# Layer 1 of a two-layer graph kernel: the last chunk's split on GpSimd, group stores at a fixed place, separate tiles for drained halves, a shorter last group

## The chip, the cores and the metric

The kernel runs on one core of a Trainium2 chip. The metric is the device time of one execution, in microseconds (us). A core has TensorE (PE in the profile) for matrix products, with its weight loads (PEld) beside them, VectorE (DVE), ScalarE (ACT) and GpSimd (POOL) for elementwise work, and SyncE (SP), which here only issues DMAs. Each engine works through its own queue in order and waits on semaphores for the others. PSUM is the memory that TensorE writes to[...].

## The reference

Two layers act on 4096 rows of 512 numbers, with a 4096 x 4096 adjacency matrix `adj` that weighs edges and masks them. Layer 0 is attention with the adjacency added to the logits; the change doesn't touch it. Layer 1 is a graph attention with 8 heads of 64:

```python
nX = (x @ W).reshape(n, NHEAD, OUT_DIM).transpose(1, 0, 2)
mean = nX.mean(-1, keepdims=True)
std = jnp.std(nX, axis=-1, ddof=1, keepdims=True)
nX = a_ln * (nX - mean) / (std + EPS) + b_ln
at1 = jnp.einsum('kno,ok->kn', nX, a1)[:, :, None]
at2 = jnp.einsum('kno,ok->kn', nX, a2)[:, :, None]
kg = at1 + at2.transpose(0, 2, 1)
kg = jax.nn.leaky_relu(kg, negative_slope=LK_ALPHA)
kg = kg * graph[None, :, :]
mg = jnp.where(mask[None, :, :], kg, NEG_FILL)
attention = jax.nn.softmax(mg, axis=-1)
y = attention @ nX + nX
y = y.transpose(1, 0, 2).reshape(n, NHEAD * OUT_DIM)
return jax.nn.elu(y)
```

Here `graph` and `mask` are `adj`, and `x` is the output of layer 0 after a layer norm and a maximum with 0. The result is added to the output of layer 0.

## The kernel before

The kernel computes both layers on a fast path without a running maximum in its softmaxes, checks ranges at the end, writes an integer `flag`, and branches to a general path if the check fails (lines 74 and 75). In the runs here the branch passes the general path by.

Layer 1 has two parts. In the first, 32 blocks of 128 rows are normalised, turned and projected (`turn`, `project`); `variance` and `standardize` divide by the deviation and give nX, the sums at1 and at2, and `own`, the rows to be added later. After each chunk of four blocks, `split` adds a constant to the sums and cuts each into three bf16 pieces, so that a product of two bf16 operands can later form at1 + at2; `sides` and `fours` turn the pieces and store them (z1_d, z2_d, u4_d). Deviations need a power -1/2, which GpSimd computes roughly, and which `standardize` refines on VectorE by five small operations. The last chunk's split doesn't fit in the first part: `split_last` spreads its 14 operations over steps 2 to 8 of the second part, two at the end of a step, and `standardize(31)` runs in the middle of step 0.

The second part is a loop of 512 steps: 8 chunks of 512 target rows (`ic`), two groups of four heads (`hg`), 32 blocks of source rows (`jt`). A group is 32 steps. Everything wrapped in `seq` stays in the order in which the program lists it, on every engine; what is not wrapped is placed by a scheduler. In step n TensorE forms the logits of the right and left heads (`sums`, lines 881 and 911; `left_sums`, line 891), VectorE and GpSimd weigh them with the adjacency (`right_leaky` 929, `right_weigh` 935, `left_weigh` 938), ScalarE takes exponentials of step n - 2 (942), and TensorE multiplies those of step n - 4 by nX (`values`, 950), into the accumulators `accs`: one tile of two halves.

Every fourth step `load_adj` issues the loads for four steps ahead on SP: pieces z2, masks nb and nx, and the weights g. Ten steps before a group ends, `open_group` loads the next group's z1 and u4, and `load_u4` the second half of u4 six steps before its end.

At the end of a group `finish` copies the two halves of `accs` to a tile `ob`, one on ScalarE and one on VectorE (965, 966), and over the next steps turns them to rows (976), divides (988, 989), adds the own rows by an accumulating DMA (1003), splits into a negative and a positive part on GpSimd, takes the exponential, and adds two more times by DMA. `close` (1018) stores the rows 21 steps after `finish` was called, that is at the end of step 24 of the next group. It isn't wrapped in `seq`.

The last group can't hide this work. For it `finish` loads the own rows and the layer's input rows to `last_in` beforehand and adds them on VectorE (1041 to 1047), in two halves with two stores (1048). Then the range check follows, not in `seq`: reductions, comparisons, two transposes on TensorE, and `flag` (1357 to 1377).

Of the kernel before, what the change touches and what calls it, by code (L numbers as in the profile page):

```python
# [24 lines left out]
SB = 4  # L25
# [54 lines left out]
def fast_path(  # L80
# [723 lines left out]
    with tc.tile_pool(name="ga_g", bufs=2) as adjs, tc.tile_pool(  # L804
# [149 lines left out]

        def finish(n, ic, hg):

            grp = groups.pop((ic, hg))
            ob = work.tile([P, 2, GC], F32, name="ob", tag="ob", bufs=1)
            y = work.tile([P, SB, 2, 2, HD], F32, name="y", tag="y", bufs=1)

            def room():
                grp["e"] = work.tile([P, SB, 2, 2, HD], F32, name="e", tag="ob", bufs=1)

            def copies():
                seq(nc.scalar.copy(ob[:, 0, :], accs[:, 0, :]))
                seq(nc.vector.tensor_copy(ob[:, 1, :], accs[:, 1, :]))  # L966

            def to_rows(hf, ks=range(2)):
                if len(ks) == 2:
                    pt = psum.tile([P, 2, GC], F32, name="pt1", tag="l", bufs=2)  # L970
                else:
                    pt = psum.tile([P, 1, GC], F32, name="pt1", tag="r1", bufs=1)
                for b in range(2 * ks[0], 2 * ks[-1] + 2):
                    col = (b % 2) * 2 * HB
                    for c in range(2):
                        seq(nc.tensor.matmul(  # L976
                            pt[ts(c, HD), b // 2 - ks[0], col : col + 2 * HB],
                            ob[:, hf, b * P + c * HD : b * P + (c + 1) * HD],
                            back.rearrange("p e c -> p (e c)"), start=True, stop=True,
                        ))  # L980
                grp["pt"] = pt[:, :, 0 : 4 * HB].rearrange("p k (b h c) -> p k b h c", h=2, c=HB)
# [35 lines left out]
            def close():  # L1017
                nc.sync.dma_start(
                    out=rows_out(ic, hg), in_=grp["e"].rearrange("p b f h e -> p b (f h e)")
                )  # L1020

            if n > n_steps:

                of_rows = [
                    last_in[0][:, 2 * k : 2 * k + 2, :].rearrange("p k c -> p (k c)").rearrange(
                        "p (b f d) -> p b f d", b=SB, f=2
                    ) for k in range(2)
                ]

                def half(t, hf):  # L1030
                    return t[:, :, hf].rearrange("p b h e -> p b (h e)")

                copies()
                to_rows(0)
                divide(0)
                to_rows(1)
                divide(1)
                room()
                e = grp["e"]
                for hf in range(2):  # L1040
                    seq(nc.vector.tensor_add(half(y, hf), half(y, hf), of_rows[0][:, :, hf]))
                    seq(nc.vector.tensor_scalar_min(half(e, hf), half(y, hf), -1.0))
                    exp_of(half(e, hf))
                    seq(nc.vector.tensor_scalar_max(half(y, hf), half(y, hf), -1.0))
                for hf, queue in enumerate((nc.sync, nc.scalar)):
                    seq(nc.vector.tensor_add(half(e, hf), half(e, hf), half(y, hf)))
                    seq(nc.vector.tensor_add(half(e, hf), half(e, hf), of_rows[1][:, :, hf]))
                    queue.dma_start(out=rows_out(ic, hg)[:, :, ts(hf, P)], in_=half(e, hf))
                return
# [23 lines left out]
        h1s = work.tile([P, 2, GC], F32, name="h1s", tag="ob", bufs=1)  # L1073
# [49 lines left out]
        def standardize(r):  # L1123
            ic, b = r // SB, r % SB
            v, root = deviating.pop(r)
# [6 lines left out]
            seq(nc.vector.reciprocal(v, w))  # L1132
            if b == 0:
                nX.append(gat.tile([P, SB, NH, HD], F32, name=f"nX{ic}"))
                owns[ic] = chunk_tile("own")
                states[ic] = prep.tile([P, SB, 2, NH], F32, name="at", tag="at", bufs=2)
# [17 lines left out]
        def split(ic):  # L1154
# [21 lines left out]
            yield lambda: seq(nc.vector.tensor_scalar_mul(at2m[:, chunk, :], at[:, :, 1, :], -4.0))  # L1176
            yield lambda: seq(nc.vector.tensor_scalar_mul(
                at1s.rearrange("p h b -> p b h"), at[:, :, 0, :], 4.0
            ))
            yield lambda: seq(nc.vector.tensor_mul(  # L1180
                at2c, at[:, :, 1, :], coef.rearrange("p b g f e -> p b (g f e)")
            ))
            for i in range(3):
                for e in range(2):
                    left = rests[e] if i else lefts_of[e]
                    yield lambda e=e, i=i, left=left: seq(
                        nc.vector.tensor_copy(piece(e, i), by_groups(left))
                    )
                    if i < 2:
                        yield lambda e=e, i=i, left=left: seq(nc.vector.tensor_sub(  # L1190
# [79 lines left out]
        for r in range(-1, NB):  # L1270
# [18 lines left out]
        def split_last():  # L1289
            pieces = split(NI - 1)  # L1290
# [15 lines left out]
        for n in range(n_steps + 4):  # L1306

            q = n // JB + 1
            if n == n_steps:

                last_in.append(work.tile([P, HG, GC], F32, name="t", tag="t", bufs=6))
# [24 lines left out]
            if done:  # L1336
# [18 lines left out]

        ends = work.tile([P, 4], F32, name="ends", tag="ends", bufs=1)
        nc.vector.tensor_reduce(ends[:, 0:1], low0, AX.X, ALU.min)
        of_all = inverses.rearrange("p i g f k q -> p (i g f k q)")
        nc.vector.tensor_reduce(ends[:, 1:2], of_all, AX.X, ALU.max)
        nc.vector.tensor_reduce(ends[:, 2:3], high0, AX.X, ALU.max)  # L1360
        nc.vector.tensor_reduce(ends[:, 3:4], of_all, AX.X, ALU.min)
        good = work.tile([P, 5], F32, name="good", tag="good", bufs=1)
        nc.vector.tensor_scalar(good[:, 0:1], ends[:, 0:1], TINY, None, ALU.is_ge)
        nc.vector.tensor_scalar(good[:, 1:2], ends[:, 1:2], 1.0 / TINY, None, ALU.is_le)
        nc.vector.tensor_scalar(good[:, 2:3], ends[:, 2:3], HUGE0, None, ALU.is_le)
        nc.vector.tensor_scalar(good[:, 3:4], ends[:, 3:4], 1.0 / HUGE1, None, ALU.is_ge)
        nc.vector.tensor_scalar_mul(ends[:, 0:1], ends[:, 0:1], SPREAD)
        nc.vector.tensor_tensor(good[:, 4:5], ends[:, 2:3], ends[:, 0:1], ALU.is_le)
        pl = psum.tile([5, P], F32, name="pl", tag="l", bufs=2)
        nc.tensor.transpose(pl, good, ident)  # L1370
        worst = work.tile([5, 1], F32, name="worst", tag="worst", bufs=1)
        nc.vector.tensor_reduce(worst, pl, AX.X, ALU.min)
        pf = psum.tile([1, 5], F32, name="pf", tag="l", bufs=2)
        nc.tensor.transpose(pf, worst, ident[:5, :5])
        every = work.tile([1, 1], F32, name="every", tag="every", bufs=1)
        nc.vector.tensor_reduce(every, pf, AX.X, ALU.min)
        nc.vector.tensor_scalar(flag, every, 0.5, None, ALU.is_lt)
# [403 lines left out]
```

## Time and profile before

| | us |
|---|---|
| median of 3 runs | 3615.72 |
| the three runs | 3607.98, 3615.72, 3619.16 |
| the profiled execution | 3612.16 |
| its span, first to last instruction | 3610.40 |

| engine | busy us | share of the span |
|---|---|---|
| PE | 3528.8 | 98% |
| PEld | 2078.8 | 58% |
| DVE | 2550.9 | 71% |
| ACT | 1745.5 | 48% |
| POOL | 2272.5 | 63% |

The profile comes from one execution. Engine times count instructions that compute; issuing a DMA and waiting don't count. Matmuls overlap one another, so a busy PE isn't a PE at its peak. Lines are those of the kernel before. A row of the timeline gives start, duration, engine, line, operation, what is written and read, and how many instructions it merges; in brackets stands the idle time just before and what ended it. Engines with a q (SPq) are their queues, which issue DMAs. In the groups, the time after the bar is busy time and the mean of one in ns, then the idle time before.

The second part of layer 1 runs from about 1994 us to 3593 us of the span, 16 groups of 32 steps. The last instruction of the check writes `flag` at 3603.5 us.

### The profile page before, as it was taken

Reading aid. Unit: us, or ns where it says so; the run is one execution under the profiler, and the core shown is the slowest. Engines: PE = TensorE matmul, PEld = TensorE weight load, DVE = VectorE, ACT = ScalarE, POOL = GpSimd, SP = SyncE. Lnnn points to the kernel's source line nnn. Section 1 sums busy time; section 2 is a strip of 40 time slices with the busy share of each in tenths; the row PEclk is TensorE's granted clock in tenths of the full one; section 3 lists DMA queues with packets and bytes.
Section 4 is the critical chain, followed back from the end, with each engine's and each line's share of the span. In section 5 each row is a group of like instructions: output and inputs, shape, how many; then the busy total and the mean of one; then the engine's idle time right before and its main releaser. Section 6 shows DMA issues by size and latency. Waiting matters only on the chain.

```text
span 3610.4 us, 58670 instructions
## 1 busy us (share of the span) xinstructions
PE 3528.8 (98%) x21482; PEld 2078.8 (58%) x21482; DVE 2550.9 (71%) x4167; ACT 1745.5 (48%) x1542; POOL 2272.5 (63%) x1802
## 2 busy tenths in 40 slices
PE   8998999999999999999999899999999999999998
PEld 3447888888888888888878222222222332222232
DVE  5435565656666565656557888888888888888887
ACT  1000111111111111111124799999999999999997
POOL 4653444444545444454557788888888888878786
PEclk9999999999999999999999999999999999999999
DMA  7567788888878888888858668877878877787885
GB/s 215 185 204 206 233 241 237 247 247 230 249 239 241 244 240 252 231 245 244 230 130 182 187 193 206 216 206 211 217 207 215 210 208 212 203 203 207 210 213 145
DMA packets 636954, 779.80 MB, mean 216 GB/s; under 512 B 78512, under 2 KB 465264, under 8 KB 627440
## 3 DMA queue, kind: packets, MB, share of 16 engines
q1 hardware_dynamic: 618800, 742.60, 72.7%
q0 software_dynamic: 16464, 31.98, 5.2%
q8 instruction: 171, 2.80, 0.3%
q10 hardware_dynamic: 1392, 1.38, 0.2%
q14 instruction: 127, 1.04, 0.1%
HBM read 593.76 MB, written 174.19 MB: 213 GB/s over the span
## 4 chain that ended last, share of the span: by engine, by line
PE 86%; DVE 8%; DMA 3%; ACT 1%; issue 1%; SPq 0%; POOL 0%; DVEq 0%; ACTq 0%; POOLq 0%
PE accs L950 23%; PE XZ L585 20%; PE M L636 20%; PE r L911 4%; PE r L881 4%; PE l L891 3%; PE pq L461 3%; PE l L911 2%; PE pv L435 2%; DVE t L938 2%; PE y L1103 1%; DMA nx<-nT_d 1%; PE pt L976 1%; DVE y L989 1%; DVE x L692 1%
## 5 line engine op out<-in xcount | busy, mean ns | idle before, releaser
L935 POOL TENSOR_TENSOR t<-t,g 128x1024 f32<-128x1024 f32 x512 | 1226.8, 2407 | 286.1 <-DVE t L929 240.2
L950 PE MATMUL accs<-t,nX 128*64 128x512 f32 x4096 | 1003.1, 605 | 4.7 <-DVE ob L966 4.7
L942 ACT ACTIVATE t<-t 128x2048 f32<-128x2048 f32 (+1 forms) x527 | 976.2, 1853 | 0.2 <-POOL t L935 0.2
L929 DVE SCALAR_TENSOR_TENSOR t<-u,at2m,r 128x512 f32<-128x512 f32 x1024 | 718.6, 743 | 190.2 <-issue 148.9
L597 ACT ACTIVATE aT<-aT 128x512 f32<-128x512 f32 x256 | 161.2, 630 | 1403.7 <-DVE aT L593 1403.7
L593 DVE TENSOR_TENSOR aT<-aT,XZ 128x256 f32<-128x256 f32 x893 | 351.9, 418 | 583.8 <-PE XZ L585 579.3
L938 DVE TENSOR_TENSOR t<-l,g 128x1024 f32<-128x1024 f32 x512 | 622.4, 1216 | 7.4 <-ACT t L942 5.4
L897 ACT ACTIVATE l<-l 128x1024 f32<-128x1024 f32 x512 | 516.3, 1008 | 132.3 <-PE l L891 82.4
L950 PEld LDWEIGHTS accs<-t,nX 128*64 128x64 f32 x4096 | 246.5, 136 | 460.3 <-issue 447.9
L585 PE MATMUL XZ<-qt,hS 128*128 128x256 f32 x2040 | 483.8, 380 | 1.9 <-DVE aT L593 1.0
L585 PEld LDWEIGHTS XZ<-qt,hS 128*128 128x128 f32 x2040 | 387.5, 190 | 57.7 <-DVE aT L593 5.1
L609 POOL TENSOR_TENSOR S<-aT 128x256 f32<-128x256 f32 x128 | 92.9, 726 | 517.9 <-ACT aT L597 517.9
L585 PE MATMUL XZ<-qt,hT 128*128 128x256 f32 x1532 | 372.5, 379 | 0.5 <-DVE aT L593 0.5
L621 POOL TENSOR_TENSOR total<-total,aT 128x256 f32<-128x256 f32 x360 | 324.1, 913 | 9.4
L585 PEld LDWEIGHTS XZ<-qt,hT 128*128 128x128 f32 x1532 | 291.0, 190 | 40.4 <-DVE aT L593 0.9
L881 PEld LDWEIGHTS <-z 6*128 6x128 bf16 x2048 | 52.4, 91 | 424.0 <-DVE t L929 353.3
L610 POOL TENSOR_TENSOR aT<-aT 128x256 f32<-128x256 f32 x128 | 93.0, 726 | 285.5 <-ACT aT L597 285.5
L636 PE MATMUL M<-v,aT 128*128 128x256 f32 x1024 | 262.8, 379 | 0.0
L636 PE MATMUL M<-tv,aT 128*128 128x256 f32 x1024 | 262.6, 379 | 0.0
L636 PE MATMUL M<-v,S 128*128 128x256 f32 x1024 | 243.3, 380 | 0.0
L577 DVE SCALAR_TENSOR_TENSOR gs<-ng,aT 128x512 f32<-128x512 bf16 x256 | 226.2, 884 | 8.8
L891 PE MATMUL l<-z_left,z 64*64 64x512 bf16 x2048 | 201.1, 380 | 17.7 <-DVE t L938 9.9
(193 smaller groups left out, 4388.7 us busy)
## 6 DMA issues: line engine op xcount, KB each, us to landing
g<-gT_d SPq DMA_DIRECT2D x128, 1024.0 KB
ag<-in_adj_dram SPq DMA_DIRECT2D x256, 256.0 KB
hS<-s_d SPq DMA_DIRECT2D x64, 1024.0 KB
gT_d<-gs SPq DMA_DIRECT2D x256, 256.0 KB
nb<-nT_d SPq DMA_DIRECT2D x128, 512.0 KB
nx<-nT_d SPq DMA_DIRECT2D x256, 256.0 KB
hT<-h_d SPq DMA_DIRECT2D x64, 768.0 KB
tv<-vt_d SPq DMA_DIRECT2D x128, 384.0 KB
```

The costliest lines, as they stand in the source:

```text
L577: seq(nc.vector.scalar_tensor_tensor(gs, ng, G_MASKED / NEG_BIG, aT, ALU.mult, ALU.add))
L585: seq(nc.tensor.matmul(out, a, b, start=start and k == 0, stop=k == 1, skip_group_check=not start,))
L593: seq(nc.vector.tensor_add(p, p, part))
L621: seq(nc.gpsimd.tensor_add(t, t, a))
L636: seq(nc.tensor.matmul(sums[ic][i][:, u, :], a[:, ts(u, P)], b, start=jt == 0 and u == 0, stop=jt == NB - 2, skip_group_check=u == 1,))
L891: seq(nc.tensor.matmul(lefts[n][ts(c, HD), r, :], loads[n // JB][2][ts(r, HD), jt % JB * P + c * HD :][:, :HD], groups[ic, hg]["z1_left"][ ...
L897: seq(nc.scalar.activation(lefts[n], lefts[n], AF.Relu, scale=4.0))
L929: seq(nc.vector.scalar_tensor_tensor(t[:, 2 + e, :], u4[:, e, :], at2m[:, jt, h : h + 1], right[e], ALU.max, ALU.add))
L935: seq(nc.gpsimd.tensor_mul(t[:, 2:4, :], t[:, 2:4, :], both_heads(n)))
L938: seq(nc.vector.tensor_mul(logits[n][:, 0:2, :], lefts.pop(n), both_heads(n)))
L942: seq(nc.scalar.activation(t, t, AF.Exp))
L950: seq(nc.tensor.matmul(accs[ts(e, HD), hf, :], nX[jt // SB][:, jt % SB, hg * HG + 2 * hf + e, :], t[:, hf + 2 * e, :], start=jt == 0, stop ...
```

## The change

Five things are changed in layer 1:

- `split` takes an engine, and for the last chunk it is GpSimd. The five operations that refine a deviation become a function of their own, `deviation`; for the last block it is called before step 0's logits are read.
- `close` is wrapped in `seq`, so that the store of a group stands on SP's queue where the program calls it.
- The tile `ob` becomes two tiles, ob0 and ob1, and the tile `e`, which shared its buffer with `ob`, gets one of its own (the early tile `h1s`, which shared it too, goes with `e`).
- In the last group each half is copied, turned, divided, and finished before the other's work is listed; a fused operation replaces a maximum and an addition; the first half is stored by ScalarE's queue and the second by SP's. The products of three late steps are listed together, by halves.
- The range check is cut in two. `check_early` runs at step 512; the inverses of the last group alone are looked at afterwards, and one product with a column of ones replaces the two transposes.

```diff
+        good = work.tile([P, 7], F32, name="good", tag="good", bufs=1)
+
+        def check_inverses(first, some):
+            ends = work.tile([P, 2], F32, name="ends", tag="ends", bufs=2)
+            seq(nc.vector.tensor_reduce(ends[:, 0:1], some, AX.X, ALU.max))
+            seq(nc.vector.tensor_reduce(ends[:, 1:2], some, AX.X, ALU.min))
+            seq(nc.vector.tensor_scalar(
+                good[:, first : first + 1], ends[:, 0:1], 1.0 / TINY, None, ALU.is_le
+            ))
+            seq(nc.vector.tensor_scalar(
+                good[:, first + 1 : first + 2], ends[:, 1:2], 1.0 / HUGE1, None, ALU.is_ge
+            ))
+
+        of_all = inverses.rearrange("p i g f k q -> p (i g f k q)")
+        of_last = of_all.shape[1] // (2 * NI)
+
+        def check_early():
+            ends = work.tile([P, 3], F32, name="ends0", tag="ends0", bufs=1)
+            seq(nc.vector.tensor_reduce(ends[:, 0:1], low0, AX.X, ALU.min))
+            seq(nc.vector.tensor_reduce(ends[:, 1:2], high0, AX.X, ALU.max))
...
+            check_inverses(3, of_all[:, : of_all.shape[1] - of_last])
+
+        def check_ranges():
+
+            check_inverses(5, of_all[:, of_all.shape[1] - of_last :])
+            pl = psum.tile([1, 7], F32, name="pl", tag="r0", bufs=1)
+            seq(nc.tensor.matmul(pl, ones, good, start=True, stop=True))
+            return pl
+
+        def set_flag(pl):
+            every = work.tile([1, 1], F32, name="every", tag="every", bufs=1)
+            seq(nc.vector.tensor_reduce(every, pl, AX.X, ALU.add))
+            seq(nc.vector.tensor_scalar(flag, every, 7.0 * P - 0.5, None, ALU.is_lt))
+
         def finish(n, ic, hg):
 
             grp = groups.pop((ic, hg))
-            ob = work.tile([P, 2, GC], F32, name="ob", tag="ob", bufs=1)
+            ob = [work.tile([P, GC], F32, name=f"ob{k}", tag=f"ob{k}", bufs=1) for k in range(2)]
             y = work.tile([P, SB, 2, 2, HD], F32, name="y", tag="y", bufs=1)
 
             def room():
-                grp["e"] = work.tile([P, SB, 2, 2, HD], F32, name="e", tag="ob", bufs=1)
+                grp["e"] = work.tile([P, SB, 2, 2, HD], F32, name="e", tag="e", bufs=1)
 
             def copies():
-                seq(nc.scalar.copy(ob[:, 0, :], accs[:, 0, :]))
-                seq(nc.vector.tensor_copy(ob[:, 1, :], accs[:, 1, :]))
+                seq(nc.scalar.copy(ob[0], accs[:, 0, :]))
+                seq(nc.vector.tensor_copy(ob[1], accs[:, 1, :]))
...
             def close():
-                nc.sync.dma_start(
+                seq(nc.sync.dma_start(
                     out=rows_out(ic, hg), in_=grp["e"].rearrange("p b f h e -> p b (f h e)")
-                )
+                ))
...
-                copies()
-                to_rows(0)
-                divide(0)
-                to_rows(1)
-                divide(1)
                 room()
                 e = grp["e"]
-                for hf in range(2):
+                for hf, queue in enumerate((nc.scalar, nc.sync)):
+                    (nc.scalar.copy, nc.vector.tensor_copy)[hf](ob[hf], accs[:, hf, :])
+                    to_rows(hf)
+                    divide(hf)
                     seq(nc.vector.tensor_add(half(y, hf), half(y, hf), of_rows[0][:, :, hf]))
                     seq(nc.vector.tensor_scalar_min(half(e, hf), half(y, hf), -1.0))
                     exp_of(half(e, hf))
-                    seq(nc.vector.tensor_scalar_max(half(y, hf), half(y, hf), -1.0))
-                for hf, queue in enumerate((nc.sync, nc.scalar)):
+                    if hf:
+                        pl = check_ranges()
+                    seq(nc.vector.scalar_tensor_tensor(
+                        half(y, hf), half(y, hf), -1.0, of_rows[1][:, :, hf], ALU.max, ALU.add
+                    ))
+                    if hf:
+                        set_flag(pl)
                     seq(nc.vector.tensor_add(half(e, hf), half(e, hf), half(y, hf)))
-                    seq(nc.vector.tensor_add(half(e, hf), half(e, hf), of_rows[1][:, :, hf]))
-                    queue.dma_start(out=rows_out(ic, hg)[:, :, ts(hf, P)], in_=half(e, hf))
+                    seq(queue.dma_start(out=rows_out(ic, hg)[:, :, ts(hf, P)], in_=half(e, hf)))
...
-        def standardize(r):
-            ic, b = r // SB, r % SB
-            v, root = deviating.pop(r)
+        def deviation(r):
+            v, root = deviating[r]
...
+        def standardize(r):
+            ic, b = r // SB, r % SB
+            v, _ = deviating.pop(r)
...
-        def split(ic):
+        def split(ic, engine=nc.vector):
...
-            yield lambda: seq(nc.vector.tensor_add(
+            yield lambda: seq(engine.tensor_add(
...
             if r >= 1:
+                deviation(r - 1)
                 standardize(r - 1)
...
+        at_step(0, deviation, NB - 1)
         later[0, "mid"] = [lambda: standardize(NB - 1)]
...
-            pieces = split(NI - 1)
+            pieces = split(NI - 1, nc.gpsimd)
...
             if n == n_steps:
 
+                check_early()
...
-            if done:
+            if done and n < n_steps + 1:
                 values(n - 4, 0)
             extra(n, "mid")
             if n < n_steps:
                 left_weigh(n)
             if done:
-                values(n - 4, 1)
+                if n < n_steps + 1:
+                    values(n - 4, 1)
                 if n % JB == 3:
                     loads.pop((n - 4) // JB)
+            if n == n_steps + 3:
+                for m, hf in ((n - 6, 0), (n - 5, 0), (n - 6, 1), (n - 5, 1)):
+                    values(m, hf)
+                for hf in range(2):
+                    values(n - 4, hf)
```

The lines of the old check at the end of the function go.

More of the change, by code (lines that the diff above doesn't have):

```diff
@@ new lines, in fast_path @@
+        of_all = inverses.rearrange("p i g f k q -> p (i g f k q)")
[4 more added lines that the diff above has]
+            seq(nc.vector.tensor_reduce(ends[:, 1:2], high0, AX.X, ALU.max))
+            seq(nc.vector.tensor_scalar(good[:, 0:1], ends[:, 0:1], TINY, None, ALU.is_ge))
+            seq(nc.vector.tensor_scalar(good[:, 1:2], ends[:, 1:2], HUGE0, None, ALU.is_le))
+            seq(nc.vector.tensor_scalar_mul(ends[:, 2:3], ends[:, 0:1], SPREAD))
+            seq(nc.vector.tensor_tensor(good[:, 2:3], ends[:, 1:2], ends[:, 2:3], ALU.is_le))
+            check_inverses(3, of_all[:, : of_all.shape[1] - of_last])
@@ L977, in to_rows @@
                             pt[ts(c, HD), b // 2 - ks[0], col : col + 2 * HB],
-                            ob[:, hf, b * P + c * HD : b * P + (c + 1) * HD],
+                            ob[hf][:, b * P + c * HD : b * P + (c + 1) * HD],
                             back.rearrange("p e c -> p (e c)"), start=True, stop=True,
@@ L1072, in fast_path @@
         xns, owns, states, ys, deviating = {}, {}, {}, {}, {}
-        h1s = work.tile([P, 2, GC], F32, name="h1s", tag="ob", bufs=1)
+        h1s = work.tile([P, 2, GC], F32, name="h1s", tag="e", bufs=1)
         sqs = work.tile([P, 2, NH, HD], F32, name="sqs", tag="y", bufs=1)
@@ L1172, in split @@
             lefts_of = {0: at[:, :, 0, :], 1: at2c}
-            yield lambda: seq(nc.vector.tensor_add(
+            yield lambda: seq(engine.tensor_add(
                 at, at, at_b.unsqueeze(1).to_broadcast([P, SB, 2, NH])
             ))
-            yield lambda: seq(nc.vector.tensor_scalar_mul(at2m[:, chunk, :], at[:, :, 1, :], -4.0))
-            yield lambda: seq(nc.vector.tensor_scalar_mul(
+            yield lambda: seq(engine.tensor_scalar_mul(at2m[:, chunk, :], at[:, :, 1, :], -4.0))
+            yield lambda: seq(engine.tensor_scalar_mul(
                 at1s.rearrange("p h b -> p b h"), at[:, :, 0, :], 4.0
             ))
-            yield lambda: seq(nc.vector.tensor_mul(
+            yield lambda: seq(engine.tensor_mul(
                 at2c, at[:, :, 1, :], coef.rearrange("p b g f e -> p b (g f e)")
@@ L1186, in split @@
                     yield lambda e=e, i=i, left=left: seq(
-                        nc.vector.tensor_copy(piece(e, i), by_groups(left))
+                        engine.tensor_copy(piece(e, i), by_groups(left))
                     )
                     if i < 2:
-                        yield lambda e=e, i=i, left=left: seq(nc.vector.tensor_sub(
+                        yield lambda e=e, i=i, left=left: seq(engine.tensor_sub(
                             by_groups(rests[e]), by_groups(left), piece(e, i)
@@ L1353, in fast_path @@
             extra(n, "end")
[L1356 to L1377, printed above, removed]
 @with_exitstack
```

## The prediction

> **What bounds the kernel now.** I read the page's chain of waits first, then its groups, then the timeline of layer 1 step by step, the waits of the SP queue, and the last 30 us.
>
> From the page:
>
> ```profile
> PE 86%; DVE 8%; DMA 3%; ACT 1%; issue 1%; SPq 0%; POOL 0%; DVEq 0%; ACTq 0%; POOLq 0%
> L935 POOL TENSOR_TENSOR t<-t,g 128x1024 f32<-128x1024 f32 x512 | 1226.8, 2407 | 286.1 <-DVE t L929 240.2
> L929 DVE SCALAR_TENSOR_TENSOR t<-u,at2m,r 128x512 f32<-128x512 f32 x1024 | 718.6, 743 | 190.2 <-issue 148.9
> ```
>
> TensorE bounds the run, and the diff gives it no less to do: two tiny transposes become one tiny product. So only places where TensorE is held up count. In layer 1 the starts of the DVE product L938, one a step, stand 2.97 us apart in the timeline while TensorE bounds. A group of 32 steps takes 98.4 us: 32 x 2.97, and 3.4 for turning the group before to rows. Two kinds of place are slower.
>
> First, the timeline of step 6, where VectorE carries the last chunk's split:
>
> ```profile
> 2020.42 0.21 DVE L1190 TENSOR_TENSOR rest<-at2c,parts 128x32 f32<-128x32 f32 x1
> ...
> 2020.55 1.40 DVE L929 SCALAR_TENSOR_TENSOR t<-u,at2m,r 128x512 f32<-128x512 f32 x2
> 2021.87 1.22 DVE L938 TENSOR_TENSOR t<-l,g 128x1024 f32<-128x1024 f32 x1
> 2022.12 2.35 POOL L935 TENSOR_TENSOR t<-t,g 128x1024 f32<-128x1024 f32 x1 [1.83 <-DVE t L929]
> 2023.00 1.56 DVE L1187 CAST parts<-rest 128x32 bf16<-128x32 f32 x1
> ```
>
> A cast of 32 elements takes 1.56 us and ends as GpSimd's product does (2024.47); elsewhere it takes 0.23. The step lasts 4.18 us and GpSimd idles 1.83 of it. L938 starts at 1999.87 in step 0, and at 2002.32, 2005.47, 2009.69, 2013.59, 2017.69, 2021.87, 2026.05, 2030.22, 2034.24 and 2036.69 in steps 1 to 10.
>
> Second, the SP queue and the chain around step 24 of group 1, and the SP queue's waits over layer 1:
>
> ```profile
> 2168.40 0.37 SPq L840 DMA_DIRECT2D g<-gT_d  x1
> 2173.69 0.38 SPq L1018 DMA_DIRECT2D out_dram<-e  x1
> 2177.59 0.36 SPq L829 DMA_DIRECT2D nb<-nT_d  x1
> 2178.04 2.91 SPq L835 DMA_DIRECT2D nx<-nT_d  x2
> ...
> 2178.67 11.10 DMA nx<-nT_d
> SPq L1018 <- DMA e<-x_d: 37.1, 15, 3.1
> SPq L829 <- DMA g<-gT_d: 15.4, 13, 1.9
> ```
>
> The store of the group before (L1018, 512 KB) waits for an accumulating DMA with the loads behind it. Eight DMAs with their eight semaphores are in flight, so the mask load nb waits until g, issued eight places earlier, has landed (2177.53 in the trace's landing records). The nx of step 28 lands 11.1 us after its issue, and g at 2193.35; GpSimd's product of step 28, which needs g, starts at 2193.51. From the same records, that product starts 0.16 us after the landing in groups 1, 5, 8, 11 and 13, and 0.5 to 5.5 us after in the others. Groups 1, 5, 11 and 13 take 100.59, 100.10, 100.47 and 100.41 us: 2.19 + 1.70 + 2.07 + 2.01 = 7.97 us over 98.4.
>
> The end, from the timeline:
>
> ```profile
> 3593.32 0.59 ACT L965 COPY ob<-accs 128x512 f32<-128x512 f32 x1 [2.98 <-PE accs L950]
> 3593.94 0.69 DVE L966 COPY ob<-accs 128x512 f32<-128x512 f32 x1 [6.97 <-ACT ob L965]
> ...
> 3597.31 0.68 DVE L1041 TENSOR_TENSOR y<-y,t 128x512 f32<-128x512 f32 x1
> ...
> 3602.75 0.14 DVE L1376 TENSOR_REDUCE every<-pf 1x1 f32<-1x5 f32 x1
> 3602.86 0.69 DVE L1047 TENSOR_TENSOR e<-e,t 128x512 f32<-128x512 f32 x1
> 3603.47 0.13 DVE L1377 TENSOR_SCALAR flag<-every 1x1 int32<-1x1 f32 x1
> ```
>
> From 3595.1 on VectorE hardly stops. When the flag is written, every engine loads it (L74, 0.48 us) and branches; SP's next record, the first wait of L75, is at 3608.17, long after the last store has landed (3606.58). So the flag on SP sets the end.
>
> **What the Trainium skill says.** GPSIMD Engine Reference, 1. Specifications: GpSimd shares its SBUF interfaces with VectorE, and they collide where VectorE runs in a two-port mode or has two SBUF inputs. The trace agrees: the 32-element operations are held, while L929 and L938, with one input in PSUM, run beside L935 at full speed. The same page, 3.1, puts GpSimd at about half VectorE's speed for two inputs (4497 ns for 2048 elements; L509 took 4514). DMA: Bandwidth & Descriptors, Queues, rings and completion order: one issuing engine's DMAs are consumed in ring order; here the landings from 2181.31 on come in SP's order of issue. TensorE: Matmul & The Clock Gate, Part 1: half clock after an idle window of 3.4 us, full again after a busy one. The windows of the trace show 0.50 from 2000 to 2012, and the clock record has it from 1996.55 to 2013.61.
>
> **The change part by part.**
>
> *The split on GpSimd and the earlier deviation.* Fourteen small operations leave VectorE in steps 2 to 8 and follow L935 on GpSimd, two a step. No row has 128x32 there. The nearest: products of 128x4 at 199 ns and 128x256 at 726 ns (a line through them gives 0.26 us), a scaling of 128x8 at 242, a copy of 128x256 at 394. I take 0.27 each. GpSimd's step is then 2.37 + 2 x 0.27 + 0.15 of gaps = 3.06 us, 0.1 over TensorE's, 0.7 us late after seven steps; that hides, since in the timeline L935 ends some 3 us before the exponential that reads it (3576.54 and 3579.79). Up to about 0.47 us each the cover holds. The dearest small operation there is pow, 1.67 us for 128x8, a different function; below 0.2 none comes. Also moved: the five operations of the last block's deviation now stand before right_leaky(0) on VectorE. Today they follow it, collide with L935 (one takes 2.27 us), and L938 of step 0 starts at 1999.87. After, they wait for GpSimd's product of block 30 (until 1996.19), then need 0.85, L929 starts at 1997.05, and L938 at about 1999.06. What is late next is the half clock: sums and L929 take turns at about 3.1 us a step, L938 at 2001.5, 2004.7, 2007.7 and 2010.8; the first values products (2.82 us at half clock) make step 5 start at 2015.5; then 2.97 each puts step 10 at 2030.4. Gain 2036.7 - 2030.4 = 6.3 us; 7.0 if the clock returns a window earlier, 2.8 if the small operations cost 0.7 each.
>
> *The store at its place.* The built order puts store and u behind the g of step 24, on SP's queue, in all 15 groups. The five loads for step 28 no longer stand behind 512 + 256 KB, which took 2181.31 - 2178.62 plus 2183.86 - 2181.31 = 5.2 us to land around the store (with other traffic between), and nb no longer waits for g; that wait falls on the second nx. By the 320 GB/s that the windows show there, 768 KB is 2.4 us at the least. Lateness of 1.7 to 2.2 us goes, 8.0 us in all; at least 6, and up to 9 with small delays such as group 8's. The next loads, for step 0 of the following group, keep the same bytes ahead; their g has at least 2.2 us to spare. The store's own wait (37.1 us in total) costs nothing at the new place, being over by then.
>
> *Separate tiles.* No gain: in the built program the VectorE copy still waits for the ScalarE copy, because both read the one accumulator tile. Old waits on stores had long been met. More room in SBUF costs nothing.
>
> *The last group.* The reordered products at steps 513 to 515 are the same 40, in a row without a gap today, so zero. VectorE after the first reciprocal (3595.11), with the starts' spacing of today's rows (reciprocal 0.21, y 0.35, addition 0.60, minimum 0.33): eight operations of divide 2.2 as before; two additions, two minima and two fused operations 0.60 + 0.33 + 0.60 each, four small range operations 0.4, the first half's closing addition 0.60, 0.15 for dependent starts; every at 3601.5, flag written at 3601.85. Two 0.60 additions and 128x256 reductions (0.33) have gone. But the second closing addition follows (to 3602.5), SP must issue its store behind it (0.38) before it loads the flag, at 2.95 instead of 3.63 past 3600: gain 0.7 us, 0.3 to 1.3. The early check's ten operations lie in VectorE's 6.97 us of idle time before 3593.94; the four removed between the layers had cover too.
>
> Sum: 6.3 + 8.0 + 0.7 = 15.0 us. The profiled execution is 3612.16 (span 3610.40), hence 3597.2. The runs' median is 3615.72, 3.6 above; from it, 3600.7. Whether those 3.6 us are more late loads, which would go too, the profile can't say. I take the middle, 3599.
>
> **The rivals.**
>
> *GpSimd becomes the bound.* For: its step has only 0.6 us to spare, the outputs are strided and in bf16. Against: small rows at 0.2. At 0.9 us each the step is today's 4.18 and the first gain shrinks to about nothing: 3605.
>
> *The late loads only move.* The store meets another load, or lateness comes from the accumulating DMAs' own traffic. Against: five groups at the very same step. Then 7.0 remain: 3607.
>
> *Slower.* The store now lands beside the loads for the next group's first steps. If writing slows reading beyond what their bytes say, those loads lose the 2.2 us that the tightest has; from there every one of 15 groups stalls as the four do now, 2.0 each. 3612.2 - 15.0 + 30 = 3627. For: queues are at 0.8 to 1.1 share there. Against: same bytes ahead as before.
>
> **How the numbers follow.** A measurement of this kernel tells 0.3% (10.8 us) from no change. Forecast 0.70 at 3599, own range 3594 to 3604; GpSimd bound 0.12; moved loads 0.13; slower 0.05. Together the range is 3593 to 3607. Faster by over 0.3% (under 3604.9): nearly all of the forecast and half of the first rival, 0.75. Slower 0.04, the rest 0.21.
>
> **What would show it.** L938 starts 2.97 apart from step 5, with POOL rows of about 0.27 at the split's lines; all groups from the second at 98.4; step 28's g landing over 2 us before its product; SP's flag load some 0.7 us earlier after the last values product. Small POOL rows above 0.5 us, a group still at 100, or a new wait on g or nx at step 0 would make it wrong.

## The result, and the profile after

| | before | after |
|---|---|---|
| median of 6 runs | 3616.39 us | 3597.57 us |
| lowest to highest | 3607.98 to 3619.72 | 3593.45 to 3598.94 |
| ratio, 95% interval | | 0.9951 [0.9936, 0.9965] |
| profiled execution, its span | 3612.16, 3610.40 | 3597.20, 3595.1 |

The median fell by 18.8 us and the profiled execution by 15.0. The difference between these two numbers is itself a finding, and the experiments explain it.

The page of the changed kernel, its chain and two of its groups (the columns behind the bars are busy us and mean ns, then idle us before and what ended it):

```profile
PE 88%; DVE 7%; DMA 2%; ACT 1%; SPq 1%; issue 1%; POOL 0%; DVEq 0%; ACTq 0%; POOLq 0%
...
L935 POOL TENSOR_TENSOR t<-t,g 128x1024 f32<-128x1024 f32 x512 | 1225.0, 2401 | 272.9 <-DVE t L929 237.0
L950 PE MATMUL accs<-t,nX 128*64 128x512 f32 x4096 | 1003.5, 606 | 4.7 <-DVE ob L1004 4.7
```

TensorE's share of the chain rose by two points and the DMA share fell by one. GpSimd's large product has 13 us less idle time in front of it. The last row is kept in mind: TensorE still waits 4.7 us in all for a VectorE copy, as before.

**The split.** The timeline of steps 5 and 6 of group 0, GpSimd first, then VectorE:

```profile
2016.72 2.37 POOL L935 TENSOR_TENSOR t<-t,g 128x1024 f32<-128x1024 f32 x1 [1.80 <-ACT l L897]
2019.04 0.32 POOL L1230 CAST parts<-at2c 128x32 bf16<-128x32 f32 x1
2019.43 0.27 POOL L1233 TENSOR_TENSOR rest<-at2c,parts 128x32 f32<-128x32 f32 x1
2019.74 2.37 POOL L935 TENSOR_TENSOR t<-t,g 128x1024 f32<-128x1024 f32 x1
2022.04 0.34 POOL L1230 CAST parts<-rest 128x32 bf16<-128x32 f32 x1
...
2018.16 1.41 DVE L929 SCALAR_TENSOR_TENSOR t<-u,at2m,r 128x512 f32<-128x512 f32 x2 [0.48 <-issue]
2019.49 1.22 DVE L938 TENSOR_TENSOR t<-l,g 128x1024 f32<-128x1024 f32 x1
```

The small operations lie between two products of GpSimd and take 0.25 to 0.34 us each. VectorE has only its two large ones. L938 starts at 2016.46, 2019.49 and 2022.45, and 2.94 to 3.03 us apart from step 5 to step 10. Group 0 takes 99.08 us instead of 104.65.

**The store.** The SP queue around step 24 of group 1, and two of its waits over layer 1 (us in total, times, longest):

```profile
2169.40 0.36 SPq L829 DMA_DIRECT2D nb<-nT_d  x1
2169.86 2.70 SPq L835 DMA_DIRECT2D nx<-nT_d  x2
2173.26 0.37 SPq L840 DMA_DIRECT2D g<-gT_d  x1
2173.73 0.46 SPq L1056 DMA_DIRECT2D out_dram<-e  x1
```

```profile
SPq L835 <- DMA g<-gT_d: 8.8, 8, 1.8
SPq L835 <- PE accs L950: 6.0, 7, 1.7
```

The store (L1056) now follows g and no longer shows up among the waits. The wait for g has passed from nb (L829) to nx (L835) and got shorter, 8.8 us for 15.4. Groups 1 to 14 take 98.41 to 98.53 us each, with no stall. In the trace's records of landings, g of step 28 now lands 2.7 to 7.1 us before the product that needs it.

**The end.** The timeline of the last 10 us:

```profile
3579.83 0.58 ACT L1074 COPY ob<-accs 128x512 f32<-128x512 f32 x1 [2.99 <-PE accs L950]
3580.45 0.69 DVE L1074 COPY ob<-accs 128x512 f32<-128x512 f32 x1 [4.73 <-ACT ob L1074]
...
3587.79 0.14 DVE L990 TENSOR_REDUCE every<-pl 1x1 f32<-1x7 f32 x1
3587.97 0.14 DVE L991 TENSOR_SCALAR flag<-every 1x1 int32<-1x1 f32 x1
3588.04 0.67 DVE L1087 TENSOR_TENSOR e<-e,y 128x512 f32<-128x512 f32 x1
3588.74 0.38 SPq L1088 DMA_DIRECT2D out_dram<-e  x1
```

The flag is complete 8.28 us after ScalarE's copy starts; before, it took 10.28. From the last L938 to the end of the span there are 22.84 us, before 24.64.

The 15.3 us of the span come from 5.57 in group 0, 7.9 in groups 1 to 14 and 1.8 at the end. The earlier deviation is not in this sum: from the last pow of the first part, L938 of step 0 comes 0.62 us sooner than before, but that pow starts 0.60 us later in this execution (1993.88 for 1993.28), so L938 starts at 1999.85 as against 1999.87.

### The profile page after: what moved, and what is told of

It is laid out like the page before. It is cut to its first block, busy times and chain, and to the rows that moved or that the text cites. A ratio compares the mean times of both kernels' runs of the same rounds, so it can differ in the third digit from the quotient of the medians.

```text
span 3595.1 us, 58674 instructions
## 1 busy us (share of the span) xinstructions
PE 3526.2 (98%) x21482; PEld 2076.9 (58%) x21482; DVE 2541.2 (71%) x4154; ACT 1745.7 (49%) x1542; POOL 2273.7 (63%) x1816
## 4 chain that ended last, share of the span: by engine, by line
PE 88%; DVE 7%; DMA 2%; ACT 1%; SPq 1%; issue 1%; POOL 0%; DVEq 0%; ACTq 0%; POOLq 0%
PE accs L950 24%; PE XZ L585 20%; PE M L636 20%; PE r L911 4%; PE r L881 4%; PE l L891 3%; PE pq L461 3%; PE l L911 3%; PE pv L435 2%; DVE t L938 2%; PE y L1143 1%; PE pt L1014 1%; DVE x L692 1%; DVE y L1027 1%; PE pa L515 0%
## 5 line engine op out<-in xcount | busy, mean ns | idle before, releaser
L929 DVE SCALAR_TENSOR_TENSOR t<-u,at2m,r 128x512 f32<-128x512 f32 x1024 | 719.4, 744 | 194.2 <-issue 151.5
L938 DVE TENSOR_TENSOR t<-l,g 128x1024 f32<-128x1024 f32 x512 | 623.6, 1218 | 0.0
L636 PEld LDWEIGHTS M<-v,S 128*128 128x128 f32 x1024 | 194.8, 191 | 26.4
```

Of the source, the lines that this page charges most:

```text
L636: seq(nc.tensor.matmul(sums[ic][i][:, u, :], a[:, ts(u, P)], b, start=jt == 0 and u == 0, stop=jt == NB - 2, skip_group_check=u == 1,))
L929: seq(nc.vector.scalar_tensor_tensor(t[:, 2 + e, :], u4[:, e, :], at2m[:, jt, h : h + 1], right[e], ALU.max, ALU.add))
L938: seq(nc.vector.tensor_mul(logits[n][:, 0:2, :], lefts.pop(n), both_heads(n)))
```

## The experiments

Each was timed beside runs of the kernel before on the same chip. Medians of different sets of runs differ by some us, so ratios count, and the traces for single steps. "Excess" is what the stalled ones among groups 1 to 14 (those over 98.6 us) take over 98.40 us each, in the profiled execution.

| kernel | median (runs) | ratio to before, 95% | excess | group 0 | last L938 to end |
|---|---|---|---|---|---|
| before (profile of the start) | | | 8.0 | 104.65 | 24.64 |
| store alone | 3605.34 (9) | 0.9969 [0.9958, 0.9980] | 0 | 104.96 | 24.72 |
| split alone | 3610.34 (22) | 0.9981 [0.9973, 0.9990] | 8.5 | 98.81 | 24.56 |
| split and deviation | 3612.26 (21) | 0.9983 [0.9974, 0.9992] | 14.3 | 98.92 | 24.60 |
| last group alone | 3616.81 (14) | 1.0002 [0.9992, 1.0012] | 16.2 | 104.67 | 22.99 |
| changed kernel again | 3597.04 (6) | 0.9949 [0.9931, 0.9967] | 0 | 99.59 | 23.06 |

The kernel before ran 53 times beside the four parts: median 3616.65, from 3603.60 to 3629.38.

**The store alone.**

```
-                nc.sync.dma_start(
+                seq(nc.sync.dma_start(
                     out=rows_out(ic, hg), in_=grp["e"].rearrange("p b f h e -> p b (f h e)")
-                )
+                ))
```

> The kernel before with one edit: the group store's place is fixed, behind the five loads for step 28. Theory (the store's place alone removes the late loads): all groups 1 to 14 take 98.4 us, group 0 still about 104.6, the time falls by 8.0 us (6 to 9). Rival (the late loads only move to step 0 of the next group or to another step): some groups still above 99.5 us and a gain under 3 us. Rival (the loads were also late in a varying way from run to run, which one profile does not show): a gain of 10 us or more between the medians, and a spread of the runs under half of that of the kernel before.

No stall is left, in any group. Yet the median fell by 11.3 us, more than the 8.0 that the profile of before shows as stalls. The last column but two of the table says why: the four profiled kernels of this table with the store at its old place lost 8.0, 8.5, 14.3 and 16.2 us to stalls, in a different set of groups each time. The runs say the same: the kernel before spreads over 26 us in 53 runs, this one over 4.7 in 9 (standard deviations 4.8 and 1.8). So the stalls are a lottery with a mean near 11 us, and the first profile had drawn a cheap execution. The third case of the expectation (10 us or more, with under half the spread) is the one that held.

**The split, without and with the earlier deviation.** In the first, `split` takes an engine and the last chunk's call gives it GpSimd. The second adds:

```
             if r >= 1:
+                deviation(r - 1)
                 standardize(r - 1)
...
+        at_step(0, deviation, NB - 1)
         later[0, "mid"] = [lambda: standardize(NB - 1)]
```

> The kernel before with one edit: the last chunk's split runs on GpSimd; the last block's deviation stays behind right_leaky(0) on VectorE. Theory (VectorE held by GpSimd's products set the step, 14 small operations of 0.3 us on GpSimd are covered): group 0 falls from 104.6 to 99.9 us, steps 5 and later 2.97 us apart, the time falls by 4.8 us; groups 1, 5, 11 and 13 still stalled at 100.1 to 100.6. Rival (the earlier deviation is needed for none of it): 5.6 us, as in the changed kernel. Rival (GpSimd becomes the bound without the earlier deviation): steps of 3.2 us or more past step 5 and a gain under 4 us.

> The kernel before with the split on GpSimd and the last block's deviation moved ahead of right_leaky(0). Theory (the two are worth 5.6 us in group 0 and stand apart from the store): group 0 at 99.1 us, the time falls by 5.6 us; against the run with the split alone, L938 of step 0 starts 0.6 to 0.8 us earlier and that difference is kept to step 10. Rival (the half clock swallows the earlier start): the same step 10 and the same time as with the split alone, within 0.2 us in the profile.

The medians fell by 6.3 and 4.4 us, but the intervals of the ratios reach some 3 us to either side, since both kernels still stall. So the gain is read from the trace, from the last pow of the first part on GpSimd to the start of L938 in step 10. Seven kernels with the split on VectorE took 43.4 to 43.7 us; the split on GpSimd alone 37.8; with the earlier deviation, in six kernels, 37.3 to 38.1. The split is worth 5.8 us. The earlier deviation starts L938 of step 0 after 5.97 us instead of 6.59, in every execution, 0.62 us sooner.

How much of this is kept past step 4 depends on when the half clock ends. Counted from the same pow, the clock records have that end at 19.7 to 21.5 us in the six, and L938 of step 5 follows in the same order, at 22.43 to 23.22. The run with the split alone had the end at 20.05 and L938 at 22.93; between the six, an end at 20.05 would give 22.6. By this estimate some 0.3 of the 0.62 us are kept, which is neither the whole, as expected, nor nothing, as in the rival. It rests on one execution without the deviation.

**The last group alone.** All edits to the last group, the range check and the tiles `ob0`, `ob1`, `e`; store and split as before.

> The kernel before with the edits to the last group, the range check and the tiles for the drained halves; store and split as before. Theory (the flag is written 2.0 us earlier after the last copy, SP stands behind its store and loads it 0.9 us earlier, and the 0.9 us less between SP's flag load and its last wait is a part of the change too): last L938 to the end of the span 22.8 us against 24.65, the time falls by 1.8 us; nothing at the boundaries of groups from the separate tiles, VectorE's copy waits 4.7 us in sum for ScalarE's as before. Rival (the shorter stretch behind the flag load came by chance): 0.7 to 0.9 us. Rival (the separate tiles also free the boundaries): 15 times 0.3 us more, 6 us in all.

The median did not move, to within some 4 us. In the trace the end is 1.65 us shorter; the medians can't confirm that, since stalls, 16.2 us in this profile, vary by more from execution to execution. At the boundaries of groups nothing changed. The end is followed up below.

**What makes the loads late.** The prediction counted two things ahead of the loads for step 28, the bytes and nb's wait for g; it showed the store's own wait with the loads behind it, and did not count it. Four kernels take these apart. The first leaves the store where it was, but loads the next group's z and the first half of its u four steps earlier, so that nb no longer shares a semaphore with g:

```
-            if n + 10 < n_steps and STEPS[n + 10][2] == 0:
-                open_group(n + 10, nc.sync)
+            if n + 14 < n_steps and STEPS[n + 14][2] == 0:
+                open_group(n + 14, nc.sync)
```

> The kernel before, with the four small loads of the next group (z_left twice, z, u) issued four steps earlier. The store keeps its place ahead of the loads for step 28 and keeps its own wait for the accumulating DMA, but g of step 24 no longer stands eight places ahead of nb, so that nb no longer waits for g; 384 KB of z and u are also gone from the stretch ahead of the loads. Theory C (nb's wait for g is what makes the loads late): all groups at 98.4 us, a median near 3605, as with the store moved, and a spread of under 6 us. Theory A (the store's own wait and its bytes ahead of the loads make them late): groups above 99.5 us remain, and the median lies within 4 us of the kernel before. Both together: a gain of some 4 to 8 us.

The second has the store moved, and two small loads in `open_group` that bring nb's wait for g back:

```
             load_u4(n, 0, queue)
+            for _ in range(2 if n else 0):
+                small = inputs.tile([6, P], BF16, name="small", tag="small", bufs=2)
+                seq(queue.dma_start(out=small, in_=z1_d[0:6, hg, ic * GC : ic * GC + P]))
```

> The kernel before with the store moved behind the loads for step 28, as in the changed kernel, and two loads of 1.5 KB each, which nothing reads, put where the store and a u load were: nb waits for g of step 24 again, eight places back, and no store stands ahead of the loads. Theory C (nb's wait for g makes the loads late): stalls at step 28 come back, groups of 100 us and more, a median within 4 us of the kernel before. Theory A (the store's wait and bytes): no stalls, 98.4 us a group, a median near 3605 to 3606.

The third and the fourth have the store moved, and at the end of step 23 one more store each: 256 bytes of e, which wait for the accumulating DMA, or all of y, which wait for nothing.

```
+                seq(nc.sync.dma_start(
+                    out=rows_out(ic, hg)[0:1, 0, 0:HD], in_=grp["e"][0:1, 0, 0, 0]
+                ))
```

> The kernel with the store moved, and at the store's old place a store of 256 bytes of the same tile e, which is written over by the real store later: SP waits there for the accumulating DMA, as before, with the loads for step 28 behind it, but next to no bytes stand ahead of them. Theory A1 (the wait holds the loads): stalls at step 28 come back, groups of 99 to 102 us, a median of 3611 to 3617. Theory A2 (the store's 512 KB ahead of the loads make them late): no stalls, a median near 3605 to 3606. Both in equal parts: near 3610.

> The kernel with the store moved, and at the store's old place a store of the tile y, 512 KB to the same rows, which the real store later writes over: y is long finished, so SP doesn't wait there, but the bytes stand ahead of the loads for step 28. Theory A2 (the bytes make the loads late): stalls at step 28 come back, a median of 3611 to 3617. Theory A1 (the wait alone does): groups of 98.4 us, a median near 3605 to 3606. The bytes are doubled for the group as a whole, so a small loss elsewhere would not tell.

Some waits of the SP queue over layer 1, of the first, the second and the third of these kernels:

```profile
SPq L1018 <- DMA e<-x_d: 68.5, 14, 6.3
...
SPq L835 <- DMA g<-gT_d: 3.3, 6, 1.0
```

```profile
SPq L825 <- DMA nx<-nT_d: 22.1, 13, 2.6
SPq L829 <- DMA g<-gT_d: 15.6, 14, 2.0
```

```profile
SPq L825 <- PE r L911: 833.4, 120, 9.7
...
SPq L1023 <- DMA e<-x_d: 41.5, 15, 3.9
```

Each kernel has the wait that it was built for. What it did to the load g of step 28, as the mean over groups 1 to 14 from issue and landing records:

| kernel | ahead of the loads | second nx, issue to landing | g, issue to landing | g landed before its use (least) | excess | median |
|---|---|---|---|---|---|---|
| before | own wait, 768 KB, nb on g | 10.4 | 11.5 | 1.2 (0.16) | 8.0 | 3616.65, 3615.11, 3615.08 |
| z, u earlier | longer own wait, 768 KB | 11.7 | 12.6 | 0.5 (0.16) | 24.8 | 3626.82 |
| nb on g | nb on g | 5.7 | 8.0 | 4.4 (2.3) | 0 | 3606.78 |
| own wait | own wait | 5.9 | 7.9 | 4.5 (3.2) | 0 | 3605.56 |
| bytes | 512 KB | 7.4 | 8.3 | 4.1 (2.9) | 0 | 3605.48 |
| store alone | none of these | 6.6 | 7.5 | 5.1 (3.1) | 0 | 3605.34 |

Read downwards: nb's wait for g is not the cause. Without it the stalls got worse (ratio 1.0035 [1.0021, 1.0048]), and brought back alone it stalls no group. The first kernel was also expected within 4 us of the kernel before if the store's wait and the bytes are the cause; it lost 11.7. Why it loses so much more is not settled: its store is reached sooner and waits 68.5 us in all instead of 33.9, while its loads are issued at about the same time in the group.

The store's wait alone stalls no group either, nor do its 512 KB alone, against both single theories: the transfers still have 2.9 us or more to spare. What stalls is what these two kernels leave out together: the wait, the 512 KB and the 256 KB of u, all in front of the loads. Whether all three are needed was not tried, but the records of issue and landing put most of it on the bytes. Times here are counted from the start of L938 in step 24. The first load (z2, L825) is never issued sooner than 4.75 us before it, because it waits for TensorE. In the kernel before it is issued then in 10 of groups 1 to 14 and up to 1.0 us later in the other four (in the first of the four kernels, with the longest wait, up to 1.8 later). The store lands at -0.1 us (mean) in the kernel before and at -0.35 in the one with the bytes, which doesn't wait. Only then do the two part: in the kernel before u lands next, at 2.4, and the five loads land 2.8 to 3.5 us later than in the other, where u stands behind them (z2 at 3.2 instead of 0.3, g at 11.5 instead of 8.05), though all but nb are issued within 0.5 us of the same place. So the 768 KB in front of the loads are the likely main cause, with the wait as a smaller part at most. A kernel with the 768 KB and no wait would show it; none was run.

**GpSimd's cover.** The changed kernel, with a subtraction of constants behind each small operation of the split:

```
+                    idle = prep.tile([P, SB, NH], F32, name="idle", tag="idle", bufs=2)
+                    seq(nc.gpsimd.tensor_sub(
+                        idle, coef.rearrange("p b g f e -> p b (g f e)"),
+                        coef.rearrange("p b g f e -> p b (g f e)"),
+                    ))
```

> The changed kernel with a 128x32 subtraction of constants on GpSimd, which nothing reads, behind each of the 14 operations of the last chunk's split: the small work of a step doubles to 1.2 us. Prediction's account (free up to 0.47 us for each of two a step, then (2c - 0.9) us a step over seven steps, with c = 0.6): some 2 us more in group 0, 101.2 us for 99.1, and 3599.7 for 3597.6. Rival (GpSimd has no cover at all, each of its late products is on the path): 14 times 0.3, 4.2 us more. Rival (the cover is deeper than that, four steps of products stand between GpSimd and the values): under 0.5 us more.

Its timeline in step 6, GpSimd alone:

```profile
2017.05 2.36 POOL L935 TENSOR_TENSOR t<-t,g 128x1024 f32<-128x1024 f32 x1
2019.36 0.33 POOL L1230 CAST parts<-rest 128x32 bf16<-128x32 f32 x1
2019.52 0.23 POOL L1242 TENSOR_TENSOR idle<-coef 128x32 f32<-128x32 f32 x1
2019.77 0.27 POOL L1233 TENSOR_TENSOR rest<-rest,parts 128x32 f32<-128x32 f32 x1
2019.99 0.24 POOL L1242 TENSOR_TENSOR idle<-coef 128x32 f32<-128x32 f32 x1
2020.19 2.38 POOL L935 TENSOR_TENSOR t<-t,g 128x1024 f32<-128x1024 f32 x1
```

Group 0 took 99.54 us, within the 99.08 and 99.59 of two executions of the changed kernel, and the median was 3594.66 (ratio 0.9942 [0.9928, 0.9955]). From step 5 to step 10 the L938s are 14.87 us apart, as in the changed kernel (14.86). There is no cost. But the dose was smaller than meant: four small operations start 0.16 to 0.25 us apart and take 0.83 together, not 1.2. The step of GpSimd is 3.14 us, 0.17 over TensorE's, and seven such steps make 1.2 us, inside the 3 us of cover. So the rival without cover fell (4.2 us). Where the cover ends wasn't reached.

**Who ends the run.** The queues of the last two stores exchanged:

```
-                for hf, queue in enumerate((nc.scalar, nc.sync)):
+                for hf, queue in enumerate((nc.sync, nc.scalar)):
```

> The changed kernel with the queues of the last group's two stores exchanged: SP issues the first half's store and loads the flag at once when it is written, ScalarE issues the second half's. Theory of the prediction (the flag on SP sets the end, because it stands behind SP's store): SP loads it 1.0 us earlier and the end comes up to 1.0 us earlier, 3596.6. Rival (the last store's landing, 4.2 us after its issue, and the engine that branches last set the end, whichever it is): no change, within 0.3 us in the profile from the last L938 product to the end (22.8 us).

From the records of SP and the landings of the last store, in us after the start of the last L938:

| | SP loads the flag | SP comes to its waits (L75) | last store issued, landed | end of span |
|---|---|---|---|---|
| before | 17.88 | 22.42 | 17.83, 20.83 | 24.64 |
| changed | 16.91 | 20.50 | 16.48, 20.70 | 22.84 |
| queues exchanged | 15.87 | 19.59 | 16.48, 20.70 | 22.84 |

With the queues exchanged SP is 0.9 us sooner at its waits and then stands there: its second wait ends at 20.72, when the store has landed. In the changed kernel that wait ends at 20.71. So in the kernel before, SP's arrival at its waits set the end, 1.6 us after the last store had landed; in the changed kernel the landing does, 0.2 us after SP's arrival, and freeing SP gives nothing more. The median (3594.98, beside 3594.66 for the kernel of the previous experiment) agrees.

**Two accumulators.** In the changed kernel the halves of `accs` are one tile. Here the first part's tile is given back at step 2 and two tiles take its place:

```
-                    accs[ts(e, HD), hf, :], nX[jt // SB][:, jt % SB, hg * HG + 2 * hf + e, :],
+                    accs[hf][ts(e, HD), :], nX[jt // SB][:, jt % SB, hg * HG + 2 * hf + e, :],
...
-                seq(nc.scalar.copy(ob[0], accs[:, 0, :]))
-                seq(nc.vector.tensor_copy(ob[1], accs[:, 1, :]))
+                seq(nc.scalar.copy(ob[0], accs[0]))
+                seq(nc.vector.tensor_copy(ob[1], accs[1]))
```

> The changed kernel with the two halves of the accumulator in tiles of their own, so that VectorE's copy of the second half no longer waits for ScalarE's of the first, nor the first product of the next group for both. Theory (that wait, 0.3 us at each of 15 boundaries, is on TensorE's path, and the separate output tiles of the change could not take it away while the accumulator was one tile): groups at 98.1 us, 4.5 us less than the changed kernel run beside it. Rival (another wait, the products' operand or VectorE's next operation, stands just behind it): under 1 us less.

Step 3 of group 2, where group 1 is drained, in the timeline of the changed kernel and then of this one:

```profile
2207.11 0.58 ACT L1003 COPY ob<-accs 128x512 f32<-128x512 f32 x1
2207.72 0.69 DVE L1004 COPY ob<-accs 128x512 f32<-128x512 f32 x1 [0.29 <-ACT ob L1003]
2208.47 1.08 PE L950 MATMUL accs<-t,nX 128*64 128x512 f32 x4 [0.31 <-DVE ob L1004]
```

```profile
2205.72 0.58 ACT L1012 COPY ob<-acc 128x512 f32<-128x512 f32 x1
2205.96 0.68 DVE L1013 COPY ob<-acc 128x512 f32<-128x512 f32 x1
2206.70 1.08 PE L959 MATMUL acc<-t,nX 128*64 128x512 f32 x4
```

VectorE's copy starts beside ScalarE's, and TensorE's wait is gone; on the page the row of the values products has 0.0 where it had 4.7. Groups take 98.02 us instead of 98.40. The end is 0.8 to 1.0 us shorter than in the two executions of the changed kernel: there ScalarE's last copy waited for the products of both halves, and now it starts 0.84 us sooner, when those of the first half are done. The median is 3589.59 (3588.38 to 3591.29, 6 runs; ratio to before 0.9929 [0.9912, 0.9947]), beside 3597.04 for the changed kernel in the same set of runs:

> The changed kernel itself, beside the others of this call, since medians of different calls differ by up to 3 us: 3595 to 3598, groups at 98.4 us, no stalls. If the sum of the parts run alone holds (store 11.3, split with deviation 4.4 to 6.3, last group 0 to 1.8 us between medians), 16 to 19 us under the kernel before.

That is 7.4 us less, where 4.5 were expected. The traces of the two show 5.4 of it between the first L938 and the last (0.39 us at a boundary, where only 0.31 had been counted as TensorE's wait) and 1.0 at the end; the last us lies within the scatter of the runs. It beats both kernels. The second line of that last expectation also held: 18.0 us under the kernel before.

## Why the prediction was right, and where its sizes were off

**The split on GpSimd (6.3 us).** Right in mechanism and close in size: 5.97 between the two profiles, 5.8 over all executions, in the range of 2.8 to 7.0. The price of 0.27 us was a little low (0.25 to 0.34), and GpSimd followed at TensorE's pace. The start of L938 was predicted 0.8 us sooner from the deviation; it was 0.62, since the sum left out 0.2 us of idle time between the last small operation and L929, which all six kernels show. The first product then waited for the half clock's end, which comes up to 1.8 us sooner or later in the six; some 0.3 us of this term are kept, by the estimate above.

**The store (8.0 us).** Right for the profile (7.9). The mechanism was half right. Of its two causes, the 768 KB ahead of the loads are the likely one, though 512 KB of them alone stall nothing; whether the store's own wait, which the prediction did not count, adds to it is open. The wait of nb for g, its second cause, stalls nothing. The new place removes all of it at once, so the number came out all the same. The mis-sized term is the step from the profile to the median: the 3.6 us between them were left open ("Whether those 3.6 us are more late loads, which would go too, the profile can't say") and half of them granted. They were late loads: the store alone is worth 11.3 us between medians. The middle of 3597.2 and 3600.7 was a guess; the lower end was right. The sum 5.8 + 11.3 + 1.8 = 18.9 agrees with the 18.8 measured (18.0 in the last set of runs).

**The sum (15.0 us).** That the profiled execution fell by just 15.0 us is in part luck: the end gave 1.1 us more than its term, and against that stood a second part that started 0.60 us later and small shortfalls elsewhere.

**Slower by late loads at step 0.** Did not happen: g of step 0 kept 2.9 to 7.1 us of slack. "The late loads only move" did not happen either.

**Separate tiles (nothing).** Right, and for the reason given: the sum of that wait is 4.7 us as before, and it went as soon as the accumulator was split.

**The last group (0.7 us).** The flag came 2.0 us sooner where 1.75 was predicted, and SP loaded it 0.96 us sooner where 0.68 was. What the sum left out is the stretch behind it: from SP's branch to its first wait took 3.8 to 4.0 us in eight kernels with the old end and 2.8 to 3.1 in six with the new one, so 1.8 us came instead of 0.7. Why it is quicker is not settled; with the old end all five engines branch within 0.4 us of each other, with the new one the engine with the last store branches 1 us behind the rest. That SP's flag sets the end was true of the kernel before; in the changed kernel the last store took over, which the prediction did not see. The reordered products and the early check cost nothing, as said: one of the check's operations was held for 1.0 us by GpSimd's product and still lay in VectorE's idle time.

**GpSimd as the bound** did not come, nor with twice the number of small operations. Two figures of this part were off in the sum itself: 3.0 us of cover over seven steps of 2.37 + 2c + 0.15 against 2.97 hold up to c = 0.44 us, not 0.47, and at 0.9 us each the step would be 4.32 us, not 4.18. Nothing rests on either.

## What to carry to other kernels

A stall that depends on when a transfer lands differs from execution to execution; where the runs of a kernel spread much more than its fixed work explains, add the spread's share to the stalls that one profile shows. Put a store that nothing waits for behind the loads on its queue, not ahead of them: here its wait alone or its 512 KB alone stalled nothing, but both, with 256 KB more, cost 11 us. When two engines drain halves of one result, split the accumulator and not only what they write to: in this build the second reader of one tile waits for the first, and each reader for the products of both halves.

## What the runs showed of the hardware

- **The start varies.** The last pow of the first part starts between 1990.4 and 1995.7 us after the start of the span in the fourteen profiles. Of this, 4.0 us of difference is there 50 us after the start, and all of it after 300 us. What is left of the spread after the stalls are gone (4.7 us for the store alone, 5.5 for the changed kernel) is of this size.
- **A wait on a queue can be free.** A store of 256 bytes that waits 41.5 us in all stands in front of the loads on SP, and no time is lost: the load behind it waits for TensorE in any case, in 13 of groups 1 to 14 until the same moment as without that store.
- **Landings need not follow the order of issue.** In the kernel before, g of step 24, of 1 MB, lands at 2177.53 us, and z_left, of 6 KB and issued 0.4 us after it, at 2176.96.
- **VectorE's small operations are still held by GpSimd's.** One of 128x8 in the deviation took 1.22 us, until GpSimd's own operation ended, and one in the early check 1.01. The Trainium skill, GPSIMD Engine Reference, 1. Specifications, names the shared interface; the lengths are those of the trace.
- **The last store takes 4.2 us or more to land** when it is issued as the other engines branch (4.22 to 4.45 in the six kernels with the new end). The last store of the old end, issued 0.6 us before the first branch, took 3.0 to 3.1, and the store before it, of the same 256 KB, 2.3.
